# A hybrid of selective scan, attention and spectral filter: Softplus for pairs of chunks, the spectral filter's narrow block first, and an x-projection in rows of eight

## The chip, the cores and the metric

The kernel runs on one core of a Trainium2 chip. A core has TensorE (matmuls), VectorE, ScalarE, GpSimd (POOL in the profile) and SyncE (SP), which here issues the transfers. Each engine works through its own instructions in program order and waits on semaphores for the others. The metric is the time of one execution on the device in microseconds; the kernel before takes 5,593.63 us, the median of three runs (5,587.63 to 5,597.10).

## The reference: what is computed

The input is four images of 48 x 48 positions (2,304 tokens) with 128 channels, all fp32. Two layers follow. Layer 0 is a selective scan (a state-space model) with a residual; layer 1 is a softmax attention with a residual and then a spectral filter ("STU") with a residual.

```python
xz = einsum('bhwc,ec->bhwe', x, in_proj_w); xin, z = split(xz)
xc = silu(depthwise_conv3x3(xin))                       # 256 channels
xs = [rows of xc, columns of xc, both reversed]         # K = 4 directions
dts, Bs, Cs = split(einsum('bkdl,kcd->bkcl', xs, x_proj_w))
dt = softplus(dts @ dt_proj_w + dt_proj_b)
h = h * exp(dt * A) + (dt * u) * B;  y = sum_n h * C    # 16 states, 2304 steps
# ... sum of directions, layer norm, gate, output projection, residual
t = t + softmax(ln(t) @ ln(t).T) @ ln(t)
# STU: causal convolutions of ln(t) with 16 filters, for 1, 1/2, 1/4 and 1/8 of the
# sequence, each times a 128 x 128 matrix per filter, plus three autoregressive taps
```

## The kernel before

**Stages.** For each image b there is a scan stage and an attention stage. During the scan stage of image b the kernel also does the STU of image b - 1; in the first scan stage it mixes the STU's matrices instead (line 934). During the attention of image b it does the prologue (projection and depthwise convolution) of image b + 1. The last image's STU stands alone at the end and is built in another way (lines 1385 to 1500).

**The scan.** Each of the four directions k is cut into six chunks of 384 tokens, so a stage has 24 chunks. k = 0 and 2 go through the image by rows, k = 1 and 3 by columns. A chunk has eight units (two halves h of the channels, four quads q of states), and a unit is one step s of the loop in `scans`. A unit has four scans on VectorE (line 511), each over 384 tokens. Before it, VectorE or GpSimd multiplies dt*u with B (line 495); ScalarE makes the decays exp(dt * A) (line 504) in a PSUM tile of the "ring"; after it, GpSimd multiplies with C (line 521) and TensorE sums over the states (line 529). VectorE then adds the sum y to the image's accumulator (line 541). The ring has five tiles in the first scan stage and four in the others; the small matmuls of the preparation borrow tiles of the same ring (`mm_hold`, `mm_done`).

**Preparation of a chunk** (`Chunk.prep`, a generator of which three pieces are run in every step). For k < 2 the x-projection (line 408) is evacuated by ScalarE into `xd` (line 413) and stored to DRAM (429); for k >= 2 `xd` is loaded back. Two matmuls make dt (422), ScalarE copies it out (425), applies Softplus in place (434), VectorE multiplies it by u (452), and SyncE stores dt and dt*u (441) in one tile `re` and loads them again, repeated over partitions, as `rep` (446). B and C come as broadcast rows `bc` (473). All these transfers stand in one queue, SyncE's. A chunk's preparation has 15 steps and begins 17 steps ahead of its first unit; `begin_scans` runs what has to be done before the first step, in the last 23 slots of the attention before it (in the first stage with nothing beside it). Softplus and Exp are in different function tables of ScalarE, so each Softplus has an ACT_TABLE_LOAD before it (shown on line 434) and one ahead of the next Exp (on line 504).

**The STU beside the scan** (`stu`). The tokens are taken as 576 groups of four. `BLOCKS` lists blocks of output groups (lo, hi, place, extra); for every block each of 16 filters is an item. An item has three convolutions, c = 0, 2, 1. Each is a series of matmuls (line 1154) with a table of shifted filter values `tt` (128 partitions by hi + 1, loaded at line 1113 into one of four buffers), one for each part of 128 groups up to hi. ScalarE copies their results: line 1170 (moves `cx` into the bank `cy`), 1177, 1178 and 1174 (into `U`). Since there is one PSUM bank for `cx` and one for `cy`, the next convolution waits for these copies. Two items later, `project` multiplies `U` with the item's matrices (line 1217); a block that crosses a border of the sequence's 1/8, 1/4 or 1/2 has two matrices (`extra`). At the end of a block the result is transposed and added to the residual `res` (line 1244), which is loaded at the block's beginning (line 1190).

**Order.** The instruction order of each engine is that in which Python emits them. `scans` interleaves the STU by counting matmul columns: each `yield` of the STU and of the preparation gives a number of columns, and `more(share)` goes on with the STU until the columns done are that share of the total. `STU_COLS` is the STU's total, `CHUNK_COLS` that of a chunk's own matmuls. Copies of the STU are emitted some 500 columns after their matmuls (`LATER`, `do_late`).

Of the kernel before, what the change touches and what calls it, by code (L numbers as in the profile page):

```python
# [8 lines left out]
F32 = mybir.dt.float32  # L9
AF = mybir.ActivationFunctionType  # L10
# [5 lines left out]
P = 128  # L16
# [21 lines left out]
SLOT = 2 * (LF + 1)  # L38


BLOCKS = [(0, 126, 0, 72), (126, 252, 1, 18), (252, 378, 2, 36), (378, 504, 3, 0), (504, 576, 3, 0)]
SHIFT = 55.0
LATER = 500

# [15 lines left out]
def hybrid_kernel(ctx: ExitStack, tc: tile.TileContext, a: dict, out: bass.AP):  # L60
# [109 lines left out]
    class Slow:  # L170


        def __init__(self, f, w):
            self.f, self.w = f, w
# [191 lines left out]
    class Chunk:  # L366


        def __init__(self, b, k, c):
            self.b, self.k, self.lo = b, k, c * CS  # L370
            self.name = f"{b}_{k}_{c}"
            self.bc, self.rep = {}, []
            self.rev = k >= 2
            self.first = c == (NCH - 1 if self.rev else 0)
            self.last = c == (0 if self.rev else NCH - 1)

            self.slot = CS if self.rev else 0
            self.at = slice(0, CS) if self.rev else slice(1, CS + 1)

        def prep(self, pool):  # L380

            k, name, xc = self.k, self.name, xcs[self.b]
            xdd_ = xdd[k % 2][self.lo // CS]

            def rest(n=1):

                yield
                yield 0
                yield
                for i in range(3 * n - 3):
                    yield 0 if i % 3 == 1 else None

            if k >= 2:
                xd = self.xd = pool.xd.tile([P, CS], F32, tag="xd", name=f"xd{name}")
                nc.sync.dma_start(xd, xdd_)
            yield from rest(2)  # L400
            if k < 2:
                hold = mm_hold()
            yield
            if k < 2:
                xd = self.xd = pool.xd.tile([P, CS], F32, tag="xd", name=f"xd{name}")
                ps = mm_tile(f"xp{name}", hold)
                for h in range(NH):
                    nc.tensor.matmul(ps[:, :CS], xw[:, h, k, :], in_order(xc[h], k, self.lo, CS),
                                     start=(h == 0), stop=(h == NH - 1))
            yield 2 * CS if k < 2 else 0  # L410
            yield
            if k < 2:
                nc.scalar.activation(xd, ps[:, :CS], AF.Identity, bias=onerow)
                mm_done(hold)
            yield from rest()

            re = pool.one.tile([P, NH, 2, CS], F32, tag="re", name=f"re{name}")
            for h in range(NH):
                hold = mm_hold()
                yield  # L420
                ps = mm_tile(f"dt{name}_{h}", hold)
                nc.tensor.matmul(ps[:, :CS], dtw[:, k, h * P:(h + 1) * P], xd, start=True, stop=True)
                yield CS
                yield
                nc.scalar.copy(re[:, h, 0], ps[:, :CS])
                mm_done(hold)
                if h == 0:
                    if k < 2:
                        nc.sync.dma_start(xdd_, xd)
                    yield from rest()  # L430
            yield
            yield 0

            nc.scalar.activation(re[:, :, 0], re[:, :, 0], AF.Softplus)
            yield
            yield
            yield 0
            d = dram.tile([NH, G4, DL, 2, CS], F32, tag="dtdu", name=f"dtdud{name}")

            def store(h):  # L440
                nc.sync.dma_start(d[h].rearrange("g j i t -> (g j) i t"), re[:, h])

            def load(h):
                rep = pool.rep.tile([P, G4, 2, CS], F32, tag="rep", name=f"rep{name}_{h}")
                for c in range(C4):
                    nc.sync.dma_start(rep[c::C4], d[h].rearrange("g j i t -> j g i t"))
                self.rep.append(rep)

            for h in range(NH):
                x = in_order(xc[h], k, self.lo, CS)  # L450
                dt, dx = [re[:, h, i].rearrange("p (r w) -> p r w", w=x.shape[2]) for i in range(2)]
                nc.vector.tensor_tensor(dx, dt, x, ALU.mult)
            yield
            yield
            store(0)
            yield 0
            store(1)
            yield
            yield from rest(2)
            load(0)  # L460
            yield from rest(2)
            yield
            yield 0
            load(1)
            yield
# [78 lines left out]
    POOLED = ((0, 3), (1, 1), (1, 3))  # L544
    order = [(k, c) for k in range(K) for c in (range(NCH) if k < 2 else reversed(range(NCH)))]
    quads = [(h, q) for h in range(NH) for q in range(Q4)]
    STEPS = 15
    LEAD = 17
    FETCHED = range(2 * Q4)

    CHUNK_COLS = len(quads) * CS + 3 * CS

    def begin_scans(b, pool):

        chunks = [Chunk(b, k, c) for k, c in order]
        preps = [ch.prep(pool) for ch in chunks]
        for i in range(7):
            next(preps[0])
        for i in range(3 * STEPS - 7):
            if next(preps[0]) is not None:  # L560
                yield
        for i in FETCHED:
            chunks[0].fetch(i, pool)
        for i in range(3 * (LEAD - len(quads))):
            if next(preps[1]) is not None:
                yield
        for i in range(3 * (LEAD - 2 * len(quads))):
            next(preps[2])
        yield chunks, preps

    def scans(b, chunks, preps, front, sp, back, ring, finish, work, work_cols):
# [39 lines left out]
        def prepare(s):  # L611

            ci, j = divmod(s, len(quads))
            for c in range(ci + 1, ci + 4):
                if c < len(chunks) and 0 <= s - len(quads) * c + LEAD < STEPS:
                    done[0] += next(preps[c]) or 0

        def refill(s, i):
# [46 lines left out]
            next(finish, None)  # L665
        for u in pending:
            u.add_y()
        assert next(work, None) is None

# [327 lines left out]
    def tail(b, J, T, po, pool, ps, last):  # L999
# [49 lines left out]
        for j in range(4):  # L1049
# [5 lines left out]
        nc.sync.dma_start(ud[:, :, 1 + P * J:1 + P * J + k], uT.rearrange("c (j p) -> c j p", j=4))  # L1055

    STU_COLS = sum(KF * 12 * sum(hi - max(lo, J * P) for J in range((hi + P - 1) // P))
                   + (2 * KF + 3) * 4 * (hi - lo) + 4 * (hi - lo) for lo, hi, place, extra in BLOCKS)

    def stu(b, env, seeds):  # L1060

# [70 lines left out]
        def conv(n, c):  # L1132

            assert seq[0] == (n, c)
            (lo, hi, place, extra), k = items[n]
            w = hi - lo
            v = w + (c != 1)
            t = tts[n, c]
            if c == 0:
                banks[0] = ps.psc.tile([P, 512], F32, tag="x", name=f"cx{b}_{n}")  # L1140
            elif 1 not in banks:
                do_late()
            p = banks.pop(1) if c == 1 else banks[0]
            p4 = p[:, :4 * v].rearrange("p (e m) -> p e m", e=4)
            nb = (hi + P - 1) // P
            for g in range(2):
                if g == 1:
                    fetch()
                first = lo - (g == 1 and c != 1)
                for J in range(nb):  # L1150
                    at = max(first, J * P) if J else first
                    end = J * P - 1
                    x = (sums[:, J, g], u[:, J, 2 + g], u[:, J, g])[c]
                    nc.tensor.matmul(p4[:, 1:3, v - (hi - at):] if g else p4[:, 0:4:3, v - (hi - at):], x,  # L1154
                                     t[:, :, hi - 1 - at + J * P:end if end >= 0 else None:-1],
                                     start=(c == 0 and J == 0 and g == 0), stop=(J == nb - 1 and g == 1),
                                     skip_group_check=(c > 0))
                    do_late(2 * (hi - at))
                    if g == 1 and J == nb - 1:
                        do_late(LATER if c == 1 else 0)  # L1160
                        later(lambda: taken(n, c, p, w))
                        seq.pop(0)
                    yield 2 * (hi - at)

        def taken(n, c, p, w):
            if c == 0:
# [13 lines left out]
        def begin(n):  # L1180
# [5 lines left out]
            nc.sync.dma_start(now["x"][:, :2, :hi - lo], ud[:, 2:, lo:hi])  # L1186
            now["mu"] = pool.one.tile([P, 2, 3, C], F32, tag="mue", name=f"mue{b}_{n}")
            nc.sync.dma_start(now["mu"][:, :m], mud[:, place:place + m])
            now["T", n] = pool.two.tile([P, 4, C], F32, tag="res", name=f"res{b}_{n}")
            nc.sync.dma_start(now["T", n][:hi - lo], td[4 * lo:4 * hi].rearrange("(p j) c -> p j c", j=4))  # L1190

        def parts(w, extra):
# [59 lines left out]
        for n, (_, k) in enumerate(items):  # L1252
            if k == 0:
                begin(n)
            yield from conv(n, 0)
            if n > 0:
                fetch_G(n - 1)
# [285 lines left out]
    run(prologue(0, turn.one, mm_tile), 3, weights(once.one))  # L1543
    turn.close()
    once.close()
    front = Stage(tc, "f0", "left", one=(1, SB), xd=(3, SB), rep=(3, SB))
    first = begun(begin_scans(0, front))
    begin0.close()
    start_y(0)
    for b in range(B):  # L1550
# [56 lines left out]
                parts.pop(0)()  # L1607
        if more:
            turn.close()
            front = Stage(tc, f"f{b + 1}", "left", one=(1, SB), xd=(3, SB), rep=(3, SB))  # L1610
            start_y(b + 1)
            pieces = begin_scans(b + 1, front)
        first = None
# [81 lines left out]
```

## Time and profile before

| what | value |
|---|---|
| median of three runs | 5,593.63 us |
| the profiled execution: its time | 5,603.98 us |
| the profiled execution: span from first to last instruction | 5,602.2 us |
| busy: TensorE, VectorE, ScalarE, GpSimd | 86%, 78%, 59%, 65% of the span |
| scans on VectorE, line 511 | 3,072 of 937 ns, 2,700.3 us |
| idle of VectorE before them | 127.2 us, of which 125.9 until a decay of line 504 |
| ACT_TABLE_LOAD on lines 434 and 504 | 95 and 89, 1,283 ns each |
| Softplus, line 434 | 96 of 844 ns |
| SyncE: issues of `rep`, `bc`, `tt`, stores of dt | 768, 3,072, 576, 192 |
| bytes moved by DMA | 1,035 MB, mean 185 GB/s |

The page divides the span into 40 slices of 140 us; a digit is the busy share of an engine in tenths. A line for a group of instructions has the line number, the engine, the operation, the tiles written and read, and the count; after the bar the busy time in us and the mean of one in ns; after the second bar how long the engine stood idle just before them and which instruction ended that idle time. "L511 <- ring L504" thus reads: the scan waited for a decay. In a list of waits the three numbers are the sum in us, the count and the longest. A timeline line has the start, the duration, the engine, the line, the operation and the tiles. Windows are in us from the span's start. The first scan runs from 120 to 1,072 us, the later scan stages from 1,320 to 2,322, 2,566 to 3,566 and 3,808 to 4,805.

### The profile page before, as it was taken

What the parts mean: (1) busy time and instruction counts of PE and PEld (TensorE: products, weight loads), DVE (VectorE), ACT (ScalarE), POOL (GpSimd) and SP (SyncE); (2) the same over time, 40 slices, a digit from 0 to 9 for tenths busy, and PEclk for the clock granted to TensorE, in tenths of its full rate; (3) what the DMA queues carried; (4) which work ended last, traced back from release to release, by engine and by line L of the source; (5) the groups of instructions that cost most, each with busy time, mean ns of one, the idle gap of its engine ahead of it and who ended that gap; (6) DMA issues with size and microseconds to landing.
All of it is one profiled execution on the core that took longest, in us unless ns stands there. A gap on an engine that the chain in (4) does not pass through costs nothing. (4 is left out here: it accounts for less than half of the span.)

```text
span 5602.2 us, 74057 instructions
## 1 busy us (share of the span) xinstructions
PE 4812.5 (86%) x23582; PEld 3078.9 (55%) x23582; DVE 4347.5 (78%) x5307; ACT 3324.9 (59%) x6923; POOL 3665.0 (65%) x1882
## 2 busy tenths in 40 slices
PE   3566556698999998898999999898999999889999
PEld 1211112345556666645666667645556667659987
DVE  6999999856899999756999999657999999513211
ACT  2777777546777776456777776457777776432111
POOL 1899999714889998505888998406889998301100
PEclk6877777799999999999999999999999999999999
DMA  3545545306887778516887778416878778226543
GB/s 104 164 151 169 169 158 166 116 30 174 237 241 249 254 253 264 167 33 195 234 250 245 250 253 278 132 59 196 247 241 254 254 251 279 73 64 155 143 146 94
DMA packets 741421, 1035.16 MB, mean 185 GB/s; under 512 B 142760, under 2 KB 564904, under 8 KB 740968
## 3 DMA queue, kind: packets, MB, share of 16 engines
q1 hardware_dynamic: 735208, 1027.13, 59.6%
q10 hardware_dynamic: 5824, 3.30, 0.3%
q8 instruction: 189, 3.10, 0.2%
q14 instruction: 200, 1.64, 0.1%
HBM read 911.77 MB, written 118.31 MB: 184 GB/s over the span
## 5 line engine op out<-in xcount | busy, mean ns | idle before, releaser
L511 DVE TENSOR_TENSOR_SCAN s<-ring,s 128x385 f32<-128x385 f32 x3072 | 2700.3, 937 | 127.2 <-ACT ring L504 125.9
L521 POOL TENSOR_TENSOR s<-s,bc 128x1536 f32<-128x1536 f32 x764 | 2429.0, 3182 | 128.2 <-DVE s L511 70.3
L504 ACT ACTIVATE ring<-rep,A 128x384 f32<-128x384 f32 x3072 | 1758.5, 584 | 795.6 <-DVE s L495 463.1
L495 POOL TENSOR_TENSOR s<-rep,bc 128x1536 f32<-128x1536 f32 x288 | 994.6, 3453 | 192.7 <-DMA bc<-xdd 155.7
L495 DVE TENSOR_TENSOR s<-rep,ring 128x1536 f32<-128x1536 f32 x480 | 831.0, 1731 | 83.0 <-issue 43.4
L529 PE MATMUL y<-s,csum 128*32 128x384 f32 x6144 | 717.5, 542 | 184.6 <-POOL s L521 117.1
L1154 PE MATMUL cx<-tt,u 128*128 128x252 f32 (+7 forms) x2880 | 622.4, 357 | 92.2 <-ACT cy L1170 90.8
L1154 PE MATMUL cx<-tt,us 128*128 128x252 f32 (+7 forms) x2880 | 626.2, 357 | 62.5 <-ACT U L1178 55.3
L1154 PEld LDWEIGHTS cx<-tt,u 128*128 128x128 f32 x2880 | 481.6, 193 | 303.9 <-ACT cy L1170 130.2
L1154 PE MATMUL cy<-tt,u 128*128 128x252 f32 (+5 forms) x2880 | 608.4, 353 | 33.3 <-DMA tt<-fd 33.2
L1154 PEld LDWEIGHTS cx<-tt,us 128*128 128x128 f32 x2880 | 481.9, 193 | 244.1 <-issue 91.9
L1154 PEld LDWEIGHTS cy<-tt,u 128*128 128x128 f32 x2880 | 484.8, 193 | 167.7 <-issue 116.3
L1217 PE MATMUL pr<-U,G 128*128 128x288 f32 (+6 forms) x1536 | 449.2, 422 | 12.0 <-DMA G<-gd 11.8
L529 PEld LDWEIGHTS y<-s,csum 128*32 128x32 f32 x6144 | 127.2, 112 | 545.3 <-issue 276.5
L1474 POOL TENSOR_TENSOR t<-s,s 128x512 f32<-128x512 f32 x48 | 63.4, 1321 | 545.9 <-ACT s L1472 545.9
L934 PE MATMUL G<-M,W 128*128 128x256 f32 (+3 forms) x512 | 235.5, 577 | 190.8 <-ACT W L924 87.3
L816 ACT ACTIVATE e<-s,shift 128x512 f32<-128x512 f32 (+1 forms) x360 | 231.2, 644 | 283.1 <-PE s L814 282.8
L814 PE MATMUL s<-xnT 128*128 128x512 f32 (+1 forms) x720 | 341.0, 558 | 13.0 <-ACT xnT L774 13.0
L806 PE MATMUL o<-e,xn 128*128 128x512 f32 (+1 forms) x720 | 337.4, 552 | 2.0 <-ACT e L816 2.0
L1217 PEld LDWEIGHTS pr<-U,G 128*128 128x128 f32 x1536 | 255.3, 192 | 137.8 <-issue 82.3
L519 POOL COPY carry<-s 128x4 f32<-128x4 f32 x640 | 122.2, 191 | 294.7 <-DVE s L511 289.3
L934 PEld LDWEIGHTS G<-M,W 128*128 128x128 f32 x512 | 104.4, 236 | 322.7 <-issue 136.8
(236 smaller groups left out, 5221.3 us busy)
## 6 DMA issues: line engine op xcount, KB each, us to landing
rep<-dtdud SPq DMA_DIRECT2D x768, 384.0 KB
bc<-xdd SPq DMA_DIRECT2D x3072, 48.0 KB
tt<-fd SPq DMA_DIRECT2D x144, 577.0 KB
dtdud<-re SPq DMA_DIRECT2D x192, 384.0 KB
tt<-fd SPq DMA_DIRECT2D x144, 505.0 KB
tt<-fd SPq DMA_DIRECT2D x144, 379.0 KB
G<-gd SPq DMA_DIRECT2D x160, 256.0 KB
t<-fd SPq DMA_DIRECT2D x80, 384.0 KB
```

The costliest lines, as they stand in the source:

```text
L495: eng.tensor_tensor(s, self.ch.rep[self.h][:, :, 1], bt.unsqueeze(1).to_broadcast([P, G4, CS]), ALU.mult)
L504: nc.scalar.activation(ring.body(self.dA[g]), ch.rep[self.h][:, g, 0], AF.Exp, scale=A[:, ch.k, self.h * G4 + g, self.q:self.q + 1])
L511: nc.vector.tensor_tensor_scan(s, ring.decays(i, ch.rev), s, 0.0, ALU.mult, ALU.add)
L519: nc.gpsimd.tensor_copy(carry[:, self.h, self.q].unsqueeze(2), self.s[:, :, end:end + 1])
L521: eng.tensor_tensor(self.s, self.s, ch.bc[Q4 + self.q].unsqueeze(1).to_broadcast([P, G4, CS]), ALU.mult)
L529: nc.tensor.matmul(ch.y[g * DL:(g + 1) * DL, :CS], csum, self.s[:, g], start=(self.q == 0), stop=(self.q == Q4 - 1))
L806: nc.tensor.matmul(po[J][:, :w], xn[:, i], e[:, :w], start=(i == 0), stop=(i == NT - 1))
L814: nc.tensor.matmul(p[:, :w], xnT[:, i * P:(i + 1) * P], xnT[:, 512 * J:512 * J + w], start=True, stop=True)
L816: nc.scalar.activation(e[:, :w], p[:, :w], AF.Exp, bias=shift)
L934: nc.tensor.matmul(p[:, :n], W[:, q if t else 0, i], M[t][:, i].unsqueeze(1).to_broadcast([P, n, C]), start=(t == 0 and i == 0), stop=(t = ...
L1154: nc.tensor.matmul(p4[:, 1:3, v - (hi - at):] if g else p4[:, 0:4:3, v - (hi - at):], x, t[:, :, hi - 1 - at + J * P:end if end >= 0 else ...
L1217: nc.tensor.matmul(o if q else o.rearrange("p f r m -> p r f m"), G, U[n][:, 4 * q:4 * q + 4, v0:v1].rearrange("p (a b) m -> p a b m", a=2 ...
```

## The change

- **Softplus for pairs.** Chunks are numbered; an even one starts 22 steps ahead in place of 17 and waits five steps before its Softplus, an odd one starts 25 ahead and waits eight steps after it, so that the Softplus of an odd chunk follows that of the even chunk before it at once. dt has a tile for even and one for odd chunks, dt*u its own, so a store of dt and dt*u is two transfers in place of one. `begin_scans` now interleaves chunks 0 and 1, and brings chunk 2 further and chunk 3 into its first pieces. `xd` has two buffers in place of three.
- **The narrow block first.** The block of 72 groups, which was the last (504 to 576), becomes the first (0 to 72), and the other four move by 72. Now two blocks have an `extra`; before there were three.
- **Copies counted.** A convolution's last yield also gives COPIES * w = 3 columns for each output group, and STU_COLS has them too. What is left of the STU after the last step is run to its end in place of an assertion.
- **x-projection in rows of eight.** For k = 1 the matmul reads 48 rows of eight neighbours in place of eight columns of 48, and the evacuation on ScalarE brings them into column order while it reads PSUM.
- **The residual** has one buffer in place of two and is loaded at the block's 15th item.

```diff
-BLOCKS = [(0, 126, 0, 72), (126, 252, 1, 18), (252, 378, 2, 36), (378, 504, 3, 0), (504, 576, 3, 0)]
+BLOCKS = [(0, 72, 0, 0), (72, 198, 1, 72), (198, 324, 2, 90), (324, 450, 3, 0), (450, 576, 3, 0)]
+COPIES = 3
...
                 for h in range(NH):
-                    nc.tensor.matmul(ps[:, :CS], xw[:, h, k, :], in_order(xc[h], k, self.lo, CS),
-                                     start=(h == 0), stop=(h == NH - 1))
+                    lo = self.lo // W
+                    x = xc[h][:, :, lo:lo + CS // H] if k else xc[h][:, lo:lo + CS // W, :]
+                    nc.tensor.matmul(ps[:, :CS], xw[:, h, k, :], x, start=(h == 0), stop=(h == NH - 1))
...
-                nc.scalar.activation(xd, ps[:, :CS], AF.Identity, bias=onerow)
+                p = ps[:, :CS]
+                if k:
+                    p = p.rearrange("p (r w) -> p w r", r=H)
+                nc.scalar.activation(xd.rearrange("p (r w) -> p r w", r=CS // W), p.rearrange("p (r w) -> p r w", w=W)
+                                     if not k else p, AF.Identity, bias=onerow)
...
-            re = pool.one.tile([P, NH, 2, CS], F32, tag="re", name=f"re{name}")
+            dt = pool.one.tile([P, NH, CS], F32, tag=f"dt{self.odd}", name=f"dt{name}")
...
-            nc.scalar.activation(re[:, :, 0], re[:, :, 0], AF.Softplus)
+            if not self.odd:
+                yield from rest(EARLY)
+            nc.scalar.activation(dt, dt, AF.Softplus)
+            if self.odd:
+                yield from rest(len(quads))
...
+            dx = pool.one.tile([P, NH, CS], F32, tag="dx", name=f"dx{name}")
...
             def store(h):
-                nc.sync.dma_start(d[h].rearrange("g j i t -> (g j) i t"), re[:, h])
+                for i, x in enumerate((dt, dx)):
+                    nc.sync.dma_start(d[h].rearrange("g j i t -> (g j) i t")[:, i], x[:, h])
...
-    STEPS = 15
-    LEAD = 17
+    EARLY = 5
+    STEPS = (15 + EARLY, 15 + len(quads))
+    LEAD = (17 + EARLY, 17 + len(quads))
...
+        DT = 23
+        for i in range(8, DT + 4):
+            go(0, min(i, DT))
+            go(1, i - 3)
+            if i % 3 != 0:
+                yield
+        go(0, DT + 3 * EARLY)
+        go(0, DT + 3 * EARLY + 1)
+        go(1, DT + 1)
+        ends = [3 * (LEAD[c % 2] - len(quads) * c) for c in range(4)]
+        ends[0] = 3 * STEPS[0]
+        yield
+        for i in range(DT + 3 * EARLY + 2, ends[0] + 1):
+            go(0, i)
+            go(2, min(i - DT - 3 * EARLY, ends[2]))
+            if i % 3 == 0:
                 yield
         for i in FETCHED:
             chunks[0].fetch(i, pool)
-        for i in range(3 * (LEAD - len(quads))):
-            if next(preps[1]) is not None:
-                yield
-        for i in range(3 * (LEAD - 2 * len(quads))):
-            next(preps[2])
+        for c in range(1, 4):
+            go(c, ends[c])
...
-            for c in range(ci + 1, ci + 4):
-                if c < len(chunks) and 0 <= s - len(quads) * c + LEAD < STEPS:
+            for c in range(ci + 1, ci + 5):
+                if c < len(chunks) and 0 <= s - len(quads) * c + LEAD[c % 2] < STEPS[c % 2]:
...
-        assert next(work, None) is None
+        for _ in work:
+            pass
...
-                   + (2 * KF + 3) * 4 * (hi - lo) + 4 * (hi - lo) for lo, hi, place, extra in BLOCKS)
+                   + KF * 3 * COPIES * (hi - lo) + (2 * KF + 3) * 4 * (hi - lo) + 4 * (hi - lo) for lo, hi, place, extra in BLOCKS)
...
-                    yield 2 * (hi - at)
+                    yield 2 * (hi - at) + (COPIES * w if g == 1 and J == nb - 1 else 0)
...
-            now["T", n] = pool.two.tile([P, 4, C], F32, tag="res", name=f"res{b}_{n}")
+
+        def residual(n):
+            (lo, hi, place, extra), k = items[n]
+            now["T", n] = pool.one.tile([P, 4, C], F32, tag="res", name=f"res{b}_{n}")
...
+            if k == KF - 2:
+                residual(n - k)
...
-            front = Stage(tc, f"f{b + 1}", "left", one=(1, SB), xd=(3, SB), rep=(3, SB))
+            front = Stage(tc, f"f{b + 1}", "left", one=(1, SB), xd=(2, SB), rep=(3, SB))
```

More of the change, by code (lines that the diff above doesn't have):

```diff
@@ L366, in hybrid_kernel, with __init__ @@
     class Chunk:
-        def __init__(self, b, k, c):
+        def __init__(self, b, i, k, c):
             self.b, self.k, self.lo = b, k, c * CS
+            self.odd = i % 2
             self.name = f"{b}_{k}_{c}"
@@ L424, in prep @@
                 yield
-                nc.scalar.copy(re[:, h, 0], ps[:, :CS])
+                nc.scalar.copy(dt[:, h], ps[:, :CS])
                 mm_done(hold)
@@ L450, in prep @@
                 x = in_order(xc[h], k, self.lo, CS)
-                dt, dx = [re[:, h, i].rearrange("p (r w) -> p r w", w=x.shape[2]) for i in range(2)]
-                nc.vector.tensor_tensor(dx, dt, x, ALU.mult)
+                v, o = [y[:, h].rearrange("p (r w) -> p r w", w=x.shape[2]) for y in (dt, dx)]
+                nc.vector.tensor_tensor(o, v, x, ALU.mult)
             yield
@@ L553, in begin_scans, with go @@
     def begin_scans(b, pool):
-        chunks = [Chunk(b, k, c) for k, c in order]
+        chunks = [Chunk(b, i, k, c) for i, (k, c) in enumerate(order)]
         preps = [ch.prep(pool) for ch in chunks]
[L557 to L560, printed above, removed]
+        calls = [0] * len(preps)
+        def go(c, n):
+            for i in range(calls[c], n):
+                next(preps[c])
+            calls[c] = n
+        DT = 23
[14 more added lines that the diff above has]
+            if i % 3 == 0:
                 yield
@@ L1545, in hybrid_kernel @@
     once.close()
-    front = Stage(tc, "f0", "left", one=(1, SB), xd=(3, SB), rep=(3, SB))
+    front = Stage(tc, "f0", "left", one=(1, SB), xd=(2, SB), rep=(3, SB))
     first = begun(begin_scans(0, front))
```

## The prediction

> **What bounds the kernel now.** I read the slices of the page first. Three scan stages of about 1,000 us (slices 9-16, 18-25, 27-34) and a first one of 950 us (slices 1-7) hold 3,950 of the 5,602 us; the change touches nothing in the last 800 us.
>
> ```profile
> PE   3566556698999998898999999898999999889999
> DVE  6999999856899999756999999657999999513211
> ACT  2777777546777776456777776457777776432111
> L511 DVE TENSOR_TENSOR_SCAN s<-ring,s 128x385 f32<-128x385 f32 x3072 | 2700.3, 937 | 127.2 <-ACT ring L504 125.9
> ```
>
> VectorE sets the scan stages, its scan waits for one thing (decays from ScalarE, 125.9 us), and TensorE is close behind. What is to be won is VectorE's idle time, so I cut the second scan stage into the spans of its STU blocks (order of columns: PE, PEld, DVE, ACT, POOL busy, PE clock, DMA share, GB/s).
>
> ```profile
> 1318.00:1565.00 247.00, 224.53 (x1104) 146.12 (x1108) 219.10 (x241) 185.42 (x404) 203.29 (x103) 0.96 0.78 226
> 1565.00:1830.00 265.00, 254.52 (x1293) 165.37 (x1286) 249.97 (x264) 193.32 (x405) 232.00 (x111) 0.97 0.79 244
> 1830.00:2110.00 280.00, 266.39 (x1374) 175.13 (x1373) 275.46 (x294) 203.03 (x424) 260.03 (x127) 1.00 0.78 251
> 2125.00:2325.00 200.00, 174.37 (x1274) 134.11 (x1272) 174.10 (x182) 117.59 (x272) 164.85 (x82) 0.96 0.76 249
> ```
>
> Idle on VectorE: 27.9, 15.0, 4.5 and 25.9 us. The two ends have different causes. In the middle of the stage the longest wait of VectorE is the first line below, at the end (2150 to 2325) the second.
>
> ```profile
> DVE s L511 <- ACT ring L504: 31.2, 28, 2.6
> DVE ya L541 <- PE y L529: 14.8, 5, 7.9
> ```
>
> The timeline shows both. At a Softplus ScalarE is shut to decays for 1.28 + 0.84 + 1.28 = 3.4 us, and the scan runs dry:
>
> ```profile
> 1402.56 1.28 ACT L434 ACT_TABLE_LOAD   x1
> 1403.85 0.84 ACT L434 ACTIVATE re<-re 128x768 f32<-128x768 f32 x1
> 1404.71 1.28 ACT L504 ACT_TABLE_LOAD   x1
> 1406.62 1.94 DVE L511 TENSOR_TENSOR_SCAN s<-ring,s 128x385 f32<-128x385 f32 x2 [2.33 <-ACT ring L504]
> ```
>
> At the end SyncE takes 9.8 us for twelve small issues, the filter table behind them is late, TensorE stands 5.2 us, and VectorE 7.9 us for the sum that is queued behind it:
>
> ```profile
> 2270.87 9.84 SPq L473 DMA_DIRECT2D bc<-xdd  x12
> 2280.80 1.04 SPq L1113 DMA_DIRECT2D tt<-fd  x2
> 2285.26 0.82 PE L1154 MATMUL cy<-tt,u 128*128 128x144 f32 x2 [5.17 <-DMA tt<-fd]
> 2294.55 0.85 DVE L541 TENSOR_TENSOR ya<-ya,y 128x384 f32<-128x384 f32 x1 [7.93 <-PE y L529]
> ```
>
> **A, the narrow block at the front.** Matmul columns of the five blocks by the formula in STU_COLS: before 42, 66, 90, 114 and 78 thousand of 390; spread over 1,000 us as the shares do, 109, 170, 231, 292 and 200 us. After, with the copies counted, 35, 74, 98, 122 and 145 thousand of 473: 73, 156, 207, 257 and 307 us. A block's tables are 49 KB times (hi + 1): the 577-wide ones are 28.4 MB in either order, over 200 us 142 GB/s, over 307 us 92. The first scan stage, with no tables, moves 160 GB/s (921 us from 150). So the end now wants 302 where its window moves 249; afterwards it wants 252, what 1830:2110 carries at 98% VectorE. Idle at the three ends (175-us windows to 2325, 3566, 4805): 25.8 + 21.4 + 21.9 = 69 us. Afterwards I expect the 2.7% of 1745-2150 (11.1 of 405 us), 4.7 us; 4 us that stay in any order (the last output's add waits 2.3 for its transposes, the last sum 1.6 for TensorE); and 2 us for a fuller TensorE: 32 in all. **-37** (bounds -55 and, see the rivals, +51).
>
> At the front nothing is won: the four copies of an item take 1.83 us at width 126 and 1.31 at 72, so the first 229 us hold 50 us of copies in either order. 0 (bounds -6 to +6).
>
> **B, Softplus in pairs.** The build has 96 table loads where before had 190: 94 x 1.283 = 121 us off ScalarE. On the path it is less. A pair shuts ScalarE for 1.28 + 2 x 0.84 + 1.28 = 4.25 us, so a pair costs the scan its old single wait plus 0.84, in place of two. If all idle of the first three windows (8 us of start aside) came from their 6, 7 and 7 Softplus, that is 3.3, 2.2 and 0.65 us each; pairs change it by 3 x (4.1 - 6.6), 3.5 x (3.0 - 4.4) and 3.5 x (1.5 - 1.3): -7.5, -4.9, +0.7, sum -11.7. If none did: 0 or a little more. I take two thirds, since the waits for the ring are 31.2 of the 45 us idle from 1345 to 2150: -7.5 a stage, **-22**. In the first scan the ring has five tiles and waits only 6.3 us in 22 Softplus; 0.84 more for each of eleven pairs is 0 to +9: **+4**.
>
> [...]
>
> **C, the x-projection.** For k = 1 a matmul record takes 822 ns and for k = 0 486: 24 chunks x 4 records x 0.336 = 32 us of TensorE, beside VectorE, worth at most some 2 us. No row shows runs of eight. [...] Nearest row: the first scan's copy to a strided target takes 808 ns in place of 472. So 0.57 becomes 0.91 us, 24 x 0.34 = 8 us on ScalarE; with no slowdown 0, with twice the time 14. On the path -2 to +4: **0**.
>
> **D, more work ahead of each later scan.** Chunk 2's projection and first dt are now inside the attention, whose end is set by TensorE (95% busy from 1150 to 1300): 3 matmuls x 2 records x 0.32 us = 1.9 us, **+6** for three. On SyncE, xdd 1 and 2, a store split in two, and chunk 2 stand before or among the loads of chunk 0, and the 32 fetches of B and C now stand behind ud<-uT: before they ran from 1291.5 to 1312.7, now from about 1304 to 1325. The first is wanted at 1314.6, when the ring is cleared, so it is in time; td, ux, fin, the fifth table and the first G queue behind them 12 us later, and TensorE's first project waits. Bounds 0 to +8 each; TensorE can be late there without VectorE: 2 each, **+6**.
>
> **E, the start.** Before the first scan nothing hides the chunks. Two projections (2.77 us at the cold clock) and two dt stand between xp and the first Softplus; TensorE's four records of dt shrink from 2.93 to 1.56 us as it stays busy: Softplus starts about 3 us later, and two more issues: **+4** (bounds +2 to +6).
>
> **F, the stores.** 192 more issues x 0.5 us = 96 us on SyncE, 1 us in each 40-us chunk, where its issues add up to 76% of 1345-2150; the repeats of dt stand behind them, half a chunk early. 0 to +5: **+1**. The residual's load moves to the 15th item, two items ahead of its use: hidden, and 2 to 5 us once for a block if not. Fewer project matmuls: same columns, 0.
>
> Sum: -37 - 22 + 4 + 0 + 12 + 4 + 1 = -38. Against the profiled execution's 5,602 us of span (5,604 with what lies around it) 5,564; that execution is 10 us above the median of the runs, so 5,593.6 - 38 = **5,556**.
>
> **Rivals.**
> 1. *ScalarE's freed time counts for more* (18 in 100). For it: copies that wait for TensorE hold up decays behind them, and those chains start at a Softplus. If the first two windows come down to the third's 1.6%, another 17 us a stage: about 5,505.
> 2. *The pairs win nothing* (15 in 100): 4.25 us is longer than the ring's four tiles (4 x 0.87 us), the first scan loses 9, and the later starts give back. Without B's 22, and +5 and +6 for these: 5,589. Against it: two waits become one.
> 3. *TensorE becomes the bound in the last block*, slower than before (7 in 100). Place: the 307 us of the 126-wide block. Its 127,200 columns at 212 ns for two records of 252 take 214 us, and 7.7 chunks of 8.7 us (eight sums of 0.85, projections) 67: 281, or 91.5%. That leaves 8.5% for its waits. If they are 14%, as the narrow block's are, each stage runs 17 us over, +51 in place of -37: 5,644. It decides from about 12.5% on. Against: the same reckoning gives 87% for the block of 1830:2110, and there VectorE idles 1.6%.
> 4. *The order of SyncE makes each scan start 8 us later* (8 in 100): 5,556 + 18 = 5,574.
>
> The forecast itself has 52 in 100. Its own range is 5,535 to 5,575. The 8-in-10 range reaches to rivals 1 and 2: 5,503 to 5,594. 0.2% (11 us) is about what this kernel's measurement can tell from no change; nearly all of the forecast, rival 1, most of rival 4 and two fifths of rival 2 lie below 5,582, rival 3 lies above 5,605: faster 0.82, same 0.12, slower 0.06.
>
> **What would show it.** A: no wait of TensorE for tt near the ends, idle there 11 us each. B: 48 loads ahead of Softplus, waits of L511's successor for the ring under 75 us in the three later scans, a little up in the first. C: the k = 1 projection near 486 ns. D, E: gaps between scan stages 2 to 4 us longer, first scan at 124. Wrong if TensorE's waits in the last block pass a tenth, or if idle at the front stays at 28.

## The result, and the profile after

The changed kernel takes 5,572.94 us (median of eleven runs, 5,566.65 to 5,582.15); the kernel before takes 5,593.63 in the same comparison. The ratio is 0.9965 (95% interval 0.9956 to 0.9975), so the change wins 20 us where 38 were forecast. It is inside the range, 17 us above the point. The profiled execution after took 5,573.41 us, 0.5 above its median, while that of before lay 10 above its own; so the two profiles differ by 30.5 us of span, and some 10 of these are not the change's.

The slices of the page after, and the scan's line of the page's groups:

```profile
PE   3666555697899999997899999897899999989999
DVE  6999999855899999855899999656899999613211
ACT  2666766545677666445777666456776666432111
L524 DVE TENSOR_TENSOR_SCAN s<-ring,s 128x385 f32<-128x385 f32 x3072 | 2696.1, 941 | 119.4 <-ACT ring L517 118.7
```

The slices hardly tell the two kernels apart; the waits for decays only fell from 125.9 to 118.7 us. The second scan stage by the spans of its blocks (columns as in the table of before; narrow block, then the 126-wide ones; the last window lies in the last block):

```profile
1330.00:1600.00 270.00, 234.69 (x1301) 164.28 (x1302) 234.17 (x261) 190.58 (x450) 218.04 (x108) 0.94 0.75 216
1600.00:1840.00 240.00, 226.25 (x1263) 155.59 (x1262) 231.78 (x246) 169.62 (x366) 217.37 (x106) 0.98 0.79 248
1840.00:2110.00 270.00, 263.84 (x1412) 175.79 (x1411) 260.67 (x280) 187.81 (x405) 247.44 (x120) 0.99 0.77 250
2137.00:2314.00 177.00, 170.00 (x932) 115.12 (x932) 173.18 (x184) 116.17 (x248) 165.29 (x79) 1.00 0.69 222
```

VectorE idles 35.8, 8.2, 9.3 and 3.8 us: the end of the stage is won (25.9 before), its front is not (27.9 of 247 before). The granted clock of TensorE in the first row is 0.94 (0.96 before); no run separates what that costs. VectorE's waits at the front (1330 to 1840):

```profile
DVE s L524 <- ACT ring L517: 24.0, 15, 5.9
DVE ya L554 <- PE y L542: 17.0, 7, 5.0
DVE s L508 <- DMA td<-T: 12.3, 1, 12.3
```

The first two lines, waits for decays and for sums, are the front's idle. The third is one wait that was 1.64 us before. It ends just before the window, at 1328.31, ahead of the first scan, so it lengthens the gap between the stages and not the front; it comes in each later stage. Taken over all stages (the scan's first and last instruction in each, computed from the two traces, us; the 24 chunks of a stage are counted from 0):

| | before | after |
|---|---|---|
| first scan starts | 120.1 | 122.5 |
| first scan stage | 951.4 | 950.1 |
| gaps from one scan stage to the next | 248.6, 244.0, 241.7 | 257.3, 254.4, 249.2 |
| scan stages 2, 3, 4 | 1002.1, 999.7, 997.1 | 984.5, 976.4, 982.4 |
| idle of VectorE in the last four chunks | 24.7, 21.4, 21.9 | 3.4, 3.4, 3.4 |
| idle in chunks 1 to 6 | 24.4, 24.6, 22.7 | 29.2, 26.5, 26.4 |

The three later scan stages win 55.6 us (58 were forecast), though up to 10 of these may be the profiled execution of before, and the gaps give back 26.6 where 12 were forecast. Most of the missing gain is in the gaps.

### The profile page after: what moved, and what is told of

The parts are those of the page before. It is cut to its first block, busy times and chain, and to the rows that moved or that the text cites. A ratio compares the mean times of both kernels' runs of the same rounds, so it can differ in the third digit from the quotient of the medians.

```text
span 5571.7 us, 73883 instructions
## 1 busy us (share of the span) xinstructions
PE 4769.3 (86%) x23372; PEld 3064.7 (55%) x23372; DVE 4326.0 (78%) x5307; ACT 3212.0 (58%) x6829; POOL 3662.0 (66%) x1882
## 5 line engine op out<-in xcount | busy, mean ns | idle before, releaser
L524 DVE TENSOR_TENSOR_SCAN s<-ring,s 128x385 f32<-128x385 f32 x3072 | 2696.1, 941 | 119.4 <-ACT ring L517 118.7
L1185 PEld LDWEIGHTS cx<-tt,u 128*128 128x128 f32 x2880 | 507.3, 194 | 337.2 <-ACT cy L1201 165.5
L1185 PE MATMUL cx<-tt,us 128*128 128x252 f32 (+7 forms) x2880 | 614.0, 355 | 43.4 <-ACT U L1209 26.5
L1185 PEld LDWEIGHTS cx<-tt,us 128*128 128x128 f32 x2880 | 494.0, 192 | 204.0 <-issue 70.9
L1251 PE MATMUL pr<-U,G 128*128 128x288 f32 (+4 forms) x1344 | 447.0, 461 | 54.3 <-DMA G<-gd 54.3
L1251 PEld LDWEIGHTS pr<-U,G 128*128 128x128 f32 x1344 | 235.9, 195 | 204.4 <-issue 80.8
```

The source lines that it names most:

```text
L524: nc.vector.tensor_tensor_scan(s, ring.decays(i, ch.rev), s, 0.0, ALU.mult, ALU.add)
L1251: nc.tensor.matmul(o if q else o.rearrange("p f r m -> p r f m"), G, U[n][:, 4 * q:4 * q + 4, v0:v1].rearrange("p (a b) m -> p a b m", a=2 ...
```

## The experiments

Theory: the parts A and B win about what the prediction says, and step D is mis-sized, because the store `td<-T` stands behind the 32 fetches of B and C in SyncE's queue and VectorE waits for it. Rivals: TensorE's added matmuls make the scans late; the pairs win nothing in the scans. Each ratio is to the kernel before as measured beside the run. The last column is that ratio's distance from 1 times 5,593.6; differences between runs are taken from it, not from the medians.

| run | what | median, us | ratio (95% interval) | us against before |
|---|---|---|---|---|
| e1 | narrow block first, alone (copies not counted) | 5,558.9 | 0.9943 (0.9931-0.9955) | -32 |
| e5 | rows of eight, alone | 5,572.9 | 0.9979 (0.9973-0.9986) | -12 |
| e9 | pairs, copies counted; old order | 5,609.5 | 1.0022 (1.0014-1.0031) | +12 |
| e2 | pairs, rows, copies counted; old order | 5,606.2 | 1.0029 (1.0017-1.0041) | +16 |
| e12 | whole change, copies not counted | 5,605.5 | 1.003 (1.0019-1.004) | +17 |
| - | whole change | 5,572.9 | 0.9965 (0.9956-0.9975) | -20 |
| e3 | whole change, early fetches of B and C | 5,536.7 | 0.9901 (0.9888-0.9914) | -55 |
| e4 | whole change, early fetch of G | 5,621.9 | 1.0057 (1.0042-1.0071) | +32 |
| e6 | before, without table switches | 5,541.8 | 0.993 (0.9908-0.9953) | -39 |
| e7 | whole change, without table switches | 5,556.2 | 0.9946 (0.993-0.9962) | -30 |
| e8 | e3, and B and C in one issue | 5,461.0 | 0.9778 (0.9764-0.9792) | -124 |
| e10 | before, and B and C in one issue | 5,507.7 | 0.9842 (0.983-0.9855) | -88 |
| e11 | e1 + e5, and B and C in one issue (copies not counted) | 5,512.1 | 0.9846 (0.9833-0.9859) | -86 |

**e3, the fetches of B and C ahead of T's store.**

```diff
         for i in range(8, DT + 4):
             go(0, min(i, DT))
             go(1, i - 3)
+            if i in (18, 20, 22, 24):
+                chunks[0].fetch((i - 18) // 2, pool)
...
         for i in range(DT + 3 * EARLY + 2, ends[0] + 1):
+            if i in (40, 41, 42, 43):
+                chunks[0].fetch(i - 36, pool)
             go(0, i)
...
-        for i in FETCHED:
-            chunks[0].fetch(i, pool)
```

> The changed kernel with the 32 fetches of chunk 0's B and C issued as soon as its x-projection is stored, ahead of the last transposed piece's store and of the last store of T. If the late start of the scans comes from T's store standing behind those fetches, each of the three gaps falls by 8 to 10 us: about 5,547 us (-26). If it comes from TensorE's added matmuls, the gaps fall by 2 us at most: 5,567 to 5,573.

The timelines of SyncE and VectorE show the cause. Before the change:

```profile
1291.49 21.24 SPq L473 DMA_DIRECT2D bc<-xdd  x32
1314.50 0.38 SPq L1022 DMA_DIRECT2D td<-T  x1
1318.48 1.75 DVE L495 TENSOR_TENSOR s<-rep,ring 128x1536 f32<-128x1536 f32 x1 [1.64 <-DMA td<-T]
```

After it:

```profile
1304.35 0.54 SPq L1086 DMA_DIRECT2D ud<-uT  x1
1305.00 20.31 SPq L486 DMA_DIRECT2D bc<-xdd  x32
1325.42 0.52 SPq L1053 DMA_DIRECT2D td<-T  x1
1328.31 1.76 DVE L508 TENSOR_TENSOR s<-rep,ring 128x1536 f32<-128x1536 f32 x1 [12.28 <-DMA td<-T]
```

And in e3:

```profile
1303.70 0.54 SPq L1088 DMA_DIRECT2D ud<-uT  x1
1312.45 0.38 SPq L1055 DMA_DIRECT2D td<-T  x1
1315.18 1.75 DVE L508 TENSOR_TENSOR s<-rep,ring 128x1536 f32<-128x1536 f32 x1 [0.39 <-DMA td<-T]
```

The attention's result T is complete at 1313.67, but its store is issued behind the 32 fetches, at 1325.42. What waits for the store is not a reader of `td`: it is VectorE's second product of the new scan, which neither reads nor writes T. In the author's reading its tile lies in memory that T held; the traces show no addresses. With the fetches moved into the attention, SyncE issues the store 13 us earlier and the wait is 0.39 us. The gaps are 246.8, 239.1 and 241.2 us, 34 less than after, and the first chunk of the first scan has also lost 11.4 of its 12.6 us of idle, while that scan starts 9.3 us later. Together -36 against the changed kernel; -26 was expected. TensorE's part in D is small: the copy of its last attention result moved from 1308.39 to 1309.97, 1.6 us, and T itself is complete no later (1314.47 before).

**e1, e5, e9, e2: the parts.** e1 is the new list BLOCKS in the kernel before and the loop in place of the assertion. e5 is the two hunks of the x-projection. e2 is the changed kernel with the old list BLOCKS. e9 is e2 with the old x-projection.

> The kernel before with the narrow block first and nothing else of the change (no copies in the portions, single Softplus). By the prediction's step A: -37, so 5,557 us. By what the trace after suggests (idle in the last four chunks of each scan stage 68 to 10 us, a little more idle at the front): -45, so about 5,549, with the three gaps between attention and scan unchanged at 249, 244 and 242 us. If the gain of the ends belongs to the pairs instead: within 10 us of 5,594.

> The kernel before with the x-projection of the odd directions in rows of eight and its re-ordered evacuation alone. By the prediction's step C: the matmul record of k = 1 falls from 822 to 486 ns, 32 us less of TensorE, and the time moves by -2 to +4: 5,592 to 5,598 us. If TensorE's 32 us count: about 5,575.

> The changed kernel with the old order of blocks and the old x-projection: pairs of Softplus, with what they bring at the starts and in the stores, alone. By the prediction's steps B, D, E and F the sum is -1: about 5,592 us against 5,594. If the parts add up as the runs with one part say (narrow order -35, rows -13, all together -21), the pairs alone cost +27: about 5,620 us, some 29 of it in the three gaps, and the later scan stages hardly shorter than before.

> The changed kernel with the old order of blocks (narrow last), all else kept: pairs, copies counted, rows of eight. By the prediction's steps B to F the sum is -1, so 5,593 us. By the theory that pairs win nothing in the later scans and that the starts cost 8 to 10 us each: about +27, so 5,620 us, with gaps of 257, 254 and 249 us.

In the order e9, e2, whole change the parts add to the result by construction: pairs with the copies counted +12, rows on top of them +4 (no difference within the intervals), the narrow block on top of both -36; sum -20. The forecast had -1, 0 and -37 for these.

e1 (expected -37 by step A) measures -32 on the time, but its idle is not where A put it: over three stages the last four chunks fall from 68.0 to 11.9 us, chunks 1 to 6 rise from 71.7 to 90.6, and the first chunk from 24.0 to 37.1.

e5 is 12 us faster alone. Its expected saving of TensorE is there (the kernel before, then e5; the x-projections that borrow a ring tile, minimum, median and maximum in ns; half of the 160 records are of k = 0):

```profile
L408 PE MATMUL ring<-xc,xw x160: 483/821/1009, 140.4 to 4198.5; 128*128 128x384 f32 x160
```

```profile
L408 PE MATMUL ring<-xc,xw x160: 482/486/1010, 138.4 to 4175.1; 128*128 128x384 f32 x160
```

Idle falls most in chunks 4 to 11 (57.2 to 40.1 us over three later stages), where the projections of chunks 6 to 11 (k = 1) are prepared. A projection holds one of the ring's four tiles, which would explain why 32 us of a TensorE that is not the bound are worth 12; that link is argued, not shown. Beside the pairs the gain is gone (e2 against e9).

In e9 the gaps are 254.0, 255.1 and 251.7 (+26.5), the first scan starts 2.5 later and its stage is 1.6 shorter; what is left of +12 is -15 for the three later scan stages. Their lengths in the profiles differ by 25, of which up to 10 may be the profiled execution of before. Since e9 counts the copies too, it does not show what the pairs alone win.

**e12, copies not counted.** COPIES = 0 in the changed kernel.

> The changed kernel with copies not counted in the portions: the narrow block is then given 62 us of a stage in place of 73, the last 327 in place of 308. If counting the copies eases the front, its idle (chunks 1 to 6, 27 us a stage) rises by 5 or more a stage: about 5,590 us. If it decides nothing, 5,568 to 5,578.

Idle rises by 9 us a stage in chunks 1 to 6 (to 37.7, 38.2 and 33.3), and by 6 in the first chunk. So with pairs and the new order, counting the copies wins 36. e12 and e2 take the same time (+1), but they differ in the order and in the counting. No run has pairs, the old order and copies not counted, so what the order alone wins beside pairs is not shown.

**e6 and e7, no table switches.** `AF.Softplus` becomes `AF.Exp` in both kernels, so dt is another number and the instruction as long as before (on line 434 of e6 a median of 846 ns, where the kernel before has 844, and no table load).

> The kernel before with every Softplus computed as an Exp instead (so dt is another number, and ScalarE switches no table for it: no loads left in the scans). By step B, which put two thirds of 40 us of idle a later stage on the single Softplus: -27 a stage and about -6 in the first scan: about 5,507 us. If other waits take their place: -30 at most, 5,565 or more.

> The changed kernel with the pairs of Softplus computed as Exp (dt is another number; no table loads left). By step B two thirds of about 28 us a later stage still stand at the pairs: -19 a stage and about -6 in the first scan: about 5,510 us, near the same change to the kernel before less what A and D are worth. If the pairs have already hidden the loads: within 10 us of 5,573.

All switches of the kernel before cost 39 us (26 to 51), half of what B implied (86). Those left in the changed kernel cost 10 (e7 against the whole change; their intervals are 9 and 5 us to each side). So the change took about 29 us off what the switches cost; e9, with the pairs, won about 15 in the later scans. A pair in the changed kernel, on ScalarE and then on VectorE:

```profile
1367.62 1.28 ACT L443 ACT_TABLE_LOAD   x1
1368.92 1.58 ACT L443 ACTIVATE dt<-dt 128x768 f32<-128x768 f32 x2
1370.60 1.28 ACT L517 ACT_TABLE_LOAD   x1
1372.58 2.66 DVE L524 TENSOR_TENSOR_SCAN s<-ring,s 128x385 f32<-128x385 f32 x3 [3.72 <-ACT ring L517]
```

ScalarE is shut to decays for 4.27 us (the next one starts at 1371.89), as worked out (4.25), and between its instructions there no gap is over 0.03 us.

**e4, G one item earlier.** For blocks with one matrix an item's G is fetched at the start of its own item; the buffers are four of half the size, so that an item with two matrices takes two issues in place of one.

```diff
+            if not any(items[i][0][3] for i in range(max(0, n - 2), n + 1)):
+                fetch_G(n)
             yield from conv(n, 0)
             if n > 0:
                 fetch_G(n - 1)
```

> The changed kernel with the combined filter weights G of blocks without a second part fetched one item earlier, from four buffers of half the size (blocks with two parts: two issues in place of one, 24 more a stage... at the old place). If late G holds the front of the stages, TensorE's wait for G (54 us in all) falls below 25 us and the idle of VectorE in chunks 1 to 6 (27 us a stage) by 4 to 8 us: 5,550 to 5,560. If the front's idle comes from the decays after a pair of Softplus, no change: 5,573.

It is 51 us slower than the changed kernel. TensorE's waits at the front (1330 to 1840), of the changed kernel and then of e4:

```profile
PE pr L1251 <- DMA G<-gd: 18.9, 10, 3.9
PE cx L1185 <- DMA tt<-fd: 6.4, 2, 5.3
```

```profile
PE cx L1186 <- DMA tt<-fd: 16.7, 9, 6.5
PE pr L1252 <- DMA G<-gd: 11.1, 7, 3.9
PE cy L1186 <- DMA tt<-fd: 4.7, 6, 1.2
```

G's waits fall by 8 us and those for the tables rise by 15; idle in chunks 1 to 6 rises from 82 to 100 us over three stages, where a fall was expected. The edit did two things: it moved issues forward, and it added 31 a stage (1,353 for 1,322). The run can't tell which made the tables late, and not all of the 51 us is accounted for. It suggested that SyncE's time to issue, not any one transfer, is what is short.

**e8, e10, e11: each fetch of B and C as one DMA.** The four rows of a fetch become four lines of one source pattern.

```diff
-            for c in range(C4):
-                row = 64 * (self.k // 2) + 32 + 4 * i + c
-                nc.sync.dma_start(t[c::C4], src[row].partition_broadcast(DL))
+            row = src[64 * (self.k // 2) + 32 + 4 * i]
+            nc.sync.dma_start(t, bass.AP(row.tensor, row.offset, [[0, DL], [CS, C4], [1, CS]]))
```

> The changed kernel with the early fetches of B and C (as in e3) and each of them as one DMA in place of four (768 issues of 192 KB instead of 3,072 of 48 KB; same bytes). If SyncE's order and issue time hold the front of the stages (late G and tables), idle in chunks 1 to 6 falls from 26 to about 12 us a stage, and the whole to about 5,495 us. If the issues are not what is short: 5,530 to 5,540, as e3. If the larger transfer lands later than four small ones and scans wait for B: slower than e3.

> The kernel before with each fetch of a row block of B and C as one DMA in place of four, nothing else: 2,304 of 3,072 issues fewer on SyncE. If SyncE's issue time is what holds both ends of the scan stages of the kernel before, idle in the last four chunks falls from 68 to below 25 us over three stages and that of chunks 1 to 6 from 72 to below 45: about 5,520 us. If the filter tables' bytes hold the ends, as step A argued (302 GB/s wanted, 249 moved), the ends keep their idle: 5,570 or more.

> The kernel before with the narrow block first, the rows of eight and each fetch of B and C as one DMA, so the run e8 without pairs (single Softplus, old order at the starts). If the pairs are worth step B's -22 once SyncE isn't short: 5,480 us or more against e8's 5,461. If pairs win nothing in the scans: no slower than e8, and 5 to 15 us faster by the earlier starts: 5,446 to 5,461.

The DMA issues of the page, of the changed kernel and of e8 (count, KB each, median us from issue to landing):

```profile
bc<-xdd SPq DMA_DIRECT2D x3072, 48.0 KB, 3.0
```

```profile
bc<-xdd SPq DMA_DIRECT2D x768, 192.0 KB, 4.3
```

Same bytes, a landing 1.3 us later, and SyncE's issues in the second scan stage add up to 409 us (43% of it) in e8, where they are 750 us (76%) in the changed kernel and 730 us (73%) in the kernel before. That alone wins 88 us in the kernel before (e10). SyncE's longest waits for a buffer of the tables (1345 to 2150), of the kernel before and then of e10, show why:

```profile
SPq L1113 <- PE cy L1154: 23.5, 15, 3.4
SPq L1113 <- PE cx L1154: 15.6, 16, 2.8
```

```profile
SPq L1112 <- PE cx L1153: 226.5, 76, 10.9
SPq L1112 <- PE cy L1153: 92.5, 40, 4.8
```

Before, the buffer was mostly free by the time SyncE came to the table; in e10 SyncE stands there and waits for it. That the transfers themselves got cheaper is a rival that the page of e10 leaves little room for: the bytes are the same, and the time of the packets is 58.7% of the span (before 59.6% of a span 94 us longer). The stage end of e10, where step A said that the tables' bytes were the limit (kernel before: 249 GB/s and 25.9 us idle in 200):

```profile
2125.00:2290.00 165.00, 154.50 (x1170) 118.89 (x1169) 156.39 (x166) 105.51 (x245) 149.02 (x73) 0.98 0.80 270
```

270 GB/s, 8.6 us idle in 165, in the old order; and where TensorE waited 11.7 us for tables from 2150 to 2325 before (the two lines below), no such wait is left in 2100 to 2290. In chunks 20 to 23 idle is 5.7, 5.7 and 5.8 us.

```profile
PE cy L1154 <- DMA tt<-fd: 10.5, 6, 5.2
PE cx L1154 <- DMA tt<-fd: 1.2, 2, 0.9
```

The front is another matter: in chunks 1 to 6 idle falls only from 72 to 61 us over three stages, where below 45 was expected. SyncE's issue time holds the ends and little of the front in the kernel before.

With SyncE relieved, narrow order and rows together win nothing (e11 against e10). The rest of the change and the early fetches win 38 more (e8 against e11 by the ratios, 51 by the medians), nearly all in the later scan stages (974.7, 978.1, 975.1 to 960.9, 959.6, 957.6), 43 us of it in the first four chunks of each. This is not the pairs alone: e8 counts the copies and e11 does not, and counting them is worth 39 us in those same chunks between e12 and the whole change. At 5,461 us e8 is the fastest, 2.2% below the kernel before.

## Why the prediction was right, and where it was wrong

The direction and the range held; the point missed by 17 us. Step D is 15 of that; the other misses (B in the later scans +7, in the first -6, C +4, E -2) nearly cancel, which is luck.

- **D failed: predicted +12, measured +26.6 in the gaps.** Its step "td, ux, fin, the fifth table and the first G queue behind them 12 us later, and TensorE's first project waits" had the delay about right (td<-T at 1314.5 before, 1325.4 after) but asked only who reads the late data. It did not ask who else waits for the late store. That is VectorE, for 12.28 us, in the author's reading because of the memory that T held. "The first is wanted at 1314.6 ..., so it is in time" was true of B and C and missed the store. TensorE's own share (1.9 predicted) was 1.6.
- **A: predicted -37, measured -32 alone (copies not counted) and -36 on top of the others; the sum is right for partly wrong reasons.** The ends fell by 56 us, not 37, and "at the front nothing is won: 0" is wrong: with single Softplus the first seven chunks lose 32 of it again. The cause is also another: not the bytes a block's tables want (302 against 249 GB/s), but SyncE's time to issue them, since e10 removes three quarters of the ends' idle with the same bytes in the same order, and the slices of its page at the three ends move 293 to 305 GB/s. (The new order also moves 39 MB less, 996 in place of 1,035 in all; what that adds in e1 is not separated.) And counting the copies, which the prediction used only to reckon durations, is worth 36 us of the whole change (e12). The prediction's own sign of being wrong, idle at the front that stays at 28, came: 35.8 us in the first 270.
- **B: predicted -22 in the later scans and +4 in the first, measured about -15 and -1.6 (e9, with the copies counted).** The loads went from 190 to 96, and two waits became one: VectorE waits for decays 105 times in the three later scans before, 67 times in e9. But the step "a pair costs the scan its old single wait plus 0.84, in place of two" is not borne out: the waits together fall only from 109.2 to 104.7 us (97.9 in the changed kernel), where the prediction's sign for B was under 75. The size was over as well: all 190 loads are worth 39 us on the path and not the 86 that "two thirds of the idle" made of them. What made e9's later scans shorter is thus not settled. In the first scan VectorE's idle rises as forecast, from 40.9 to 46.4 us; the stage is still shorter because the products dt*u on VectorE take 54.1 us in place of 61.1 there, which the prediction had at nothing (e9 has 53.6; the reason is not shown). The pair at 1367.62 shut ScalarE for 4.27 us where 4.25 were reckoned; that much held.
- **C: predicted 0, and 0 within the intervals beside the pairs; -12 alone, outside its bounds of -2 to +4.** That TensorE's 32 us are "worth at most some 2 us" failed in e5. That a matmul reading runs of 32 bytes would be as fast as that of k = 0, on which the 486 ns and the 32 us rest, no run of before shows; e5 does: the median of its records is 486 ns, where it was 821. The evacuation did not slow down: 564 ns after, reading PSUM in steps of 32 bytes, 571 before. The 0.91 us was reckoned from a copy to a strided target (808 ns in place of 472) and did not carry over to this strided source.
- **E: predicted +4, measured +2.4. F: predicted +1,** inside the -15 of B and not separable from it; of the moved residual only a wait of 1.4 us for its transposes is left at the end of the second scan stage. The cold clock of E was a granted clock of 0.50 (before, 96.98 to 99.80 us, the 2.77 us of projections) and of 1.00 from 100.42 to 102.00, where the four records of dt took 1.56 us.
- **The rivals.** The fourth came true, in place and size: each scan starts 7.5 to 10.4 us later by SyncE's order, and its 5,574 is the time measured to within 1.1 us. It had 8 in 100. That close a hit is luck in part: it has +30 for D where the gaps give 26.6, and -22 and +4 for B. The third did not decide: in the last block TensorE is 96% busy (170.00 of 177 us), more than the 91.5 reckoned, and VectorE still only idles 3.8 us in it. The first (freed ScalarE counts more) did not show here: the front's idle rose. The second is not refuted: e9's later scans are shorter, but e9 counts the copies too, and VectorE's waits for decays hardly fell in it. Only the worth of the switches, 39 us before and 10 after, speaks for the pairs. Its 5,589 is 16 us above the time measured.

## What to carry to other kernels

When a transfer is moved in a queue, list who waits for everything queued behind it, and count a late store like a late load: here VectorE, which does not read it, waited 12.28 us for one. Add up the issue time of a queue before blaming bytes or an engine that waits for data; at three quarters full it cost 88 us here. Fetching one load earlier in more pieces only made others late, whereas issuing the same bytes of B and C in a quarter as many DMAs won the 88 us. Parts of a change that ease the same shortage don't add: the narrow order is worth 32 us alone, and nothing (with rows of eight) once SyncE is relieved.

## What was not expected of the hardware

- An issue of B and C took SyncE 0.58 us on average in the second scan stage with 48 KB (changed kernel) and 0.59 with 192 KB (e8); the broadcast of 192 KB landed in 4.3 us (e8) where one of 48 KB landed in 3.0 (changed kernel).
- ScalarE's 128x384 evacuation from PSUM took 564 ns with a source in steps of 32 bytes (changed kernel) and 571 without (kernel before), though the same engine's copy to a strided target took 808 in place of 472 (line 539 of the kernel before, from 430 to 680 us).
- The x-projection's matmul with its moving operand in runs of 32 bytes (e5) took as long as with contiguous rows, 486 ns; in steps of 192 bytes (kernel before) it took 822.
